# A two-layer graph network on one core: the order of work in layer 0's rounds, in layer 1's node steps, and at the end of both layers

## The chip, the core and the metric

The kernel runs on one core of a Trainium2 chip. The metric is the device time of one execution in microseconds (us); smaller is better. The engines are named as the profile names them: PE (matrix products and transposes), DVE (vector engine), ACT (scalar engine with activation tables), POOL (here it issues the gathers) and SP (it issues nearly all other DMAs). Each engine works through its own instructions strictly in the order in which they were written down, and waits where an operand isn't ready.

## What is computed

6250 nodes with 128 features, 106250 edges sorted by destination. Layer 0 is an attention layer (GATv2), layer 1 a mean of edge messages with a gate. Cut to what matters:

```python
h  = relu(layernorm(x))
xl = h @ Wl + bl ; xr = h @ Wr + br
m  = leaky_relu(xl[src] + xr[dst] + edge_attr @ We, 0.2)
logits = m @ att
ex = exp(logits - segment_max(logits, dst)[dst])
agg = segment_sum(xl[src] * (ex / segment_sum(ex, dst)[dst]), dst)
x  = x + batchnorm(gelu(h + agg + bias_out))          # batch norm: over all nodes

h  = relu(layernorm(x))
em = relu(layernorm(concat(h[src], h[dst]) @ msg_w + msg_b)) * edge_weight
messages = segment_sum(em, dst) / (count + 1e-8)
g  = sigmoid(h @ gate_w + gate_b)
x  = x + g * relu(layernorm(concat(h, messages) @ upd_w + upd_b)) + (1 - g) * h
```

## The kernel before, in words

**Blocks and rounds.** The edges are cut into 104 blocks (`NS`) of 1024 edges, 8 tiles (`ST`) of 128 edges. Both layers run a loop of one round per block `s`. In each round POOL issues eight indirect DMAs (`gather`, L200) that fetch the source rows of 1024 edges from a table in HBM; PE spreads the destination rows to the edges by a product with a one-hot matrix (`expand`, L895; the one-hot comes from `one_hot_t`: a product into `dlp` at L890 and a comparison into `oht` at L891); and a block's sum by destination is again a product with a one-hot matrix (`oh`). That sum is copied out of PSUM and stored to HBM (`flush`, `store` at L898) in one of two tables, by the parity of the block.

**Layer 0's round** (L1056 on). The newest block `s`: DVE adds the gathered rows to the spread rows in PSUM (L1072), ACT takes Relu (L1073), DVE multiplies by the attention vector (L1098), reduces to logits (L1100) and puts them into `lgc` (L1101 to L1104). Behind it, the lagging block `u = s - 7` (`LAG` = 7): its one-hot `oh` (L1079, DVE), the copy of two extra columns (L1082), eight weightings of gathered rows with the softmax numerators (L1094, ACT; after the last gather every second one on DVE, L1092), and the product into `agg_ps` (L1110), which has a single PSUM buffer. `flush(u - 1)` empties that buffer (L1046). Gathered rows have 10 buffers.

**Maxima.** Every fourth round a generator `maxima(b)` (L936) starts. It takes the maximum of the logits over each destination for 4 blocks in eight steps, two per round: a transpose of the logits (L940), scans on DVE (L943 to L948), small transposes (L951, L952), scans of one row, transposes (L966), scans and Exp (L969 to L974), transposes back (L977, L978), and the result `exm` (L982, L984) that the weighting of these 4 blocks reads. Its PSUM tiles share the buffer `mx` with `dlp`.

**Node groups of layer 0** (`nodes`, L989). 13 groups of 4 nodes tiles (the last two have 3 and 2). A group starts when its edges have been stored (`due`), and takes one step per round: load both tables (L904); two empty steps; the maxima and an Exp (L1001 to L1006); the combine and transposes (L1009 to L1022); the bias and Gelu (L1024, L1026); the statistics of the batch norm (L1028). Group 11 starts at round 109; group 12, the last, after the loop. `both(group, nodes(12))` runs the two in turn, one step of each, the last group first. After them come the batch norm's scale (L1150 to L1158, with a Sqrt at L1151), and the stage that makes layer 1's tables.

**Layer 1's round** (L1323 on). DVE adds gathered and spread rows (`y`, L1338); ACT squares the eight tiles with a sum (L1343) and takes Sqrt (L1344); `flush1`; for the block before, `u = s - 1`: one-hot (L1349), scaling (L1354, eight), a bias (L1356) on DVE, Relu (L1357) and weighting (L1360, eight) on ACT; the product into `agg1_ps` (L1370, single buffer). Gathered rows have 6 buffers.

**Node groups of layer 1** (`nodes1`, L1248), again one step per round at the end of the round: load; an empty step; the mean of messages (L1258 to L1266); transposes into `nt` and a copy (L1273, L1274); products into `nz` and, in the same step, their reading into `z` (L1278 to L1281); statistics and Sqrt (L1287 to L1290); scaling (L1292 to L1295); the rest on DVE with transposes of `h` into `nt` and of `x` into `nz` (L1298 to L1311); the output's DMA (L1314). `nt` and `nz` are single buffers of one PSUM bank; `nt` is also the buffer of layer 1's `dlp`. Group 10 starts at round 97, group 11 at round 103, group 12 after the loop; when a group is due, the one before it is finished first, with all the steps that are left.

The order of work is written out by hand (`manual_schedule`): within a layer each engine gets its instructions in the order of the source.

## Time and profile before

| | |
|---|---|
| median of 3 runs | 2320.14 us (2317.82 to 2320.94) |
| time of the profiled execution | 2316.21 us |
| its span, first to last instruction | 2314.1 us |
| granted PE clock, mean | 0.807 |
| busy: POOL, DVE, PE, ACT | 1611.4, 1766.5, 1437.2, 1273.6 us |
| last gather of layer 0 issued at | 1104.39 us |
| first and last gather of layer 1 issued at | 1216.66, 2256.41 us |

How to read the profile. A line of a group reads: line, engine, operation, output<-input, count | busy us, mean ns of one | idle time of the engine just before it, and what ended most of it. A line in order of time reads: start in us, duration in us, engine, line, operation, output<-input, shape, count, and in brackets the idle time before it and its releaser. The busy table by stage has one row per stretch of time: the busy us of PE, PE's weight loads, DVE, ACT and POOL, then the granted PE clock, the share of the DMA engines, and GB/s. Consecutive instructions of one line are merged in the view in order of time.

### The profile page before, as it was taken

The numbers are of one execution on the slowest core, as the hardware profiler recorded it, in microseconds if no ns is written. First come the engines' busy times: TensorE is split into PE (matmuls) and PEld (weight loads), VectorE is DVE, ScalarE is ACT, GpSimd is POOL, SyncE is SP. The second block draws the span as 40 slices with busy tenths as digits, with TensorE's granted clock in tenths as the row PEclk, the third lists the DMA queues.
The fourth block names the chain that finished last, engine by engine and source line by source line (L and its number), as shares of the span: only waits on it lengthen the run. The fifth ranks groups of instructions, "written<-read, shape, count | busy, mean of one in ns | idle before, by whom it ended". The sixth has DMA issues, their size and how long they took to land.

```text
span 2314.1 us, 30585 instructions
## 1 busy us (share of the span) xinstructions
PE 1437.2 (62%) x8206; PEld 1245.6 (54%) x8206; DVE 1766.5 (76%) x3795; ACT 1273.6 (55%) x4208; POOL 1611.4 (70%) x1703
## 2 busy tenths in 40 slices
PE   5656666566656666666585666666665666566663
PEld 4545555455555555556464555555555555555553
DVE  5578788788788788777655777797797887788786
ACT  5224344443344344443465776777777777777674
POOL 1777777777777777777037777777777777777770
PEclk9679878887787878887787777888888788888886
DMA  5742343332332332332132222232233233233231
GB/s 149 179 132 68 87 142 107 76 76 67 76 77 67 76 77 67 77 76 66 40 112 61 67 76 75 70 80 78 68 80 80 64 80 81 66 81 79 67 79 28
DMA packets 187647, 188.13 MB, mean 81 GB/s; under 512 B 38256, under 2 KB 154960, under 8 KB 187464
## 3 DMA queue, kind: packets, MB, share of 16 engines
q0 software_dynamic: 53792, 110.57, 19.8%
q1 hardware_dynamic: 130812, 75.25, 11.3%
q8 instruction: 66, 1.08, 0.2%
q10 hardware_dynamic: 2860, 0.27, 0.1%
q14 instruction: 117, 0.96, 0.1%
HBM read 142.91 MB, written 43.04 MB: 80 GB/s over the span
## 4 chain that ended last, share of the span: by engine, by line
POOL 31%; DVE 25%; issue 14%; DMA 12%; PE 10%; ACT 6%; DVEq 0%; POOLq 0%; ACTq 0%; another core or an unknown queue 0%; SPq 0%
POOL gl L200 31%; DMA gl<-xl_d,src_c 8%; DVE y L1354 4%; DMA gl<-a_d,src_c 3%; PE agg_ps L1370 3%; DVE m_ps L1072 3%; DVE y L1338 2%; DVE oh L1349 2%; DVE y L1356 2%; ACT sq L1343 2%; DVE oht L891 2%; ACT y L1357 1%; ACT glw L1360 1%; PE mm L1203 1%; DVE lr L1100 1%
## 5 line engine op out<-in xcount | busy, mean ns | idle before, releaser
L200 POOL DMA_INDIRECT gl<-xl_d,src_c x832 | 790.6, 950 | 298.8 <-issue 230.4
L200 POOL DMA_INDIRECT gl<-a_d,src_c x832 | 787.4, 946 | 261.0 <-issue 226.2
L1370 PEld LDWEIGHTS agg_ps<-glw,oh 128*128 128x128 f32 x1664 | 314.3, 272 | 481.6 <-ACT glw L1360 481.6
L890 PE MATMUL dlp<-dl_b,ident_b 104*128 104x512 bf16 x416 | 179.3, 431 | 607.4 <-DVE oht L891 500.1
L1110 PEld LDWEIGHTS agg_ps<-glw,oh 128*128 128x128 f32 x1664 | 295.8, 267 | 228.6 <-ACT glw L1094 209.8
L1370 PE MATMUL agg_ps<-glw,oh 128*128 128x129 f32 x1664 | 341.1, 382 | 90.7 <-ACT glw L1360 81.3
L891 DVE TENSOR_SCALAR oht<-dlp,iota_p 126x512 f32<-126x512 f32 x416 | 309.7, 744 | 97.9 <-PE dlp L890 97.9
L1343 ACT ACTIVATE sq<-y 128x128 f32<-128x128 f32 x832 | 256.9, 309 | 225.3 <-DVE y L1338 202.4
L1073 ACT ACTIVATE m_ps<-m_ps 128x1024 f32<-128x1024 f32 x104 | 104.9, 1008 | 501.1 <-DVE m_ps L1072 249.3
L1110 PE MATMUL agg_ps<-glw,oh 128*128 128x130 f32 x1664 | 299.1, 355 | 22.6 <-ACT glw L1094 10.5
L895 PE MATMUL m_ps<-W,oht 128*128 128x128 f32 x1664 | 255.5, 317 | 12.1 <-DMA oht<-in_edge_weight_dram 6.2
L1072 DVE TENSOR_TENSOR m_ps<-m_ps,gl 128x1024 f32<-128x1024 f32 x104 | 128.0, 1231 | 173.6 <-DMA gl<-xl_d,src_c 164.5
L1360 ACT ACTIVATE glw<-y,ew_c 128x128 f32<-128x128 f32 x832 | 254.5, 389 | 3.4
L895 PEld LDWEIGHTS m_ps<-W,oht 128*128 128x128 f32 x1664 | 238.5, 229 | 20.8 <-DVE lr L1100 11.0
L1094 ACT ACTIVATE glw<-gl,exm 128x128 f32<-128x128 f32 x804 | 245.9, 393 | 0.1
L895 PEld LDWEIGHTS y_ps<-W,oht 128*128 128x128 f32 x1664 | 223.4, 216 | 8.9 <-issue 7.2
L895 PE MATMUL y_ps<-W,oht 128*128 128x128 f32 x1664 | 227.0, 295 | 0.0
L1354 DVE SCALAR_TENSOR_TENSOR y<-y,rs,cst 128x128 f32<-128x128 f32 x832 | 223.2, 340 | 0.0
L1338 DVE TENSOR_TENSOR y<-y_ps,gl 128x1024 f32<-128x1024 f32 x104 | 125.3, 1205 | 47.4 <-DMA gl<-a_d,src_c 45.7
L1343 ACT ACTIVATION_READ_ACCUMULATOR sq<-y 128x1 f32 x832 | 155.0, 186 | 0.0
L1357 ACT ACTIVATE y<-y 128x1024 f32<-128x1024 f32 x104 | 109.9, 1056 | 44.2 <-DVE y L1356 44.2
L1100 DVE TENSOR_REDUCE lr<-m_ps 128x8 f32<-128x1024 f32 x104 | 127.3, 1224 | 3.6
(255 smaller groups left out, 1769.2 us busy)
## 6 DMA issues: line engine op xcount, KB each, us to landing
gl<-xl_d,src_c POOLq DMA_INDIRECT x832
gl<-a_d,src_c POOLq DMA_INDIRECT x832
res<-agg SPq DMA_DIRECT2D x104, 64.0 KB
res<-agg SPq DMA_DIRECT2D x104, 63.5 KB
W<-xr_d SPq DMA_DIRECT2D x104, 63.0 KB
W<-b_d SPq DMA_DIRECT2D x104, 63.0 KB
res<-zt SPq DMA_DIRECT2D x20, 325.0 KB
res<-zt SPq DMA_DIRECT2D x20, 322.5 KB
```

What stands on the lines that cost most here:

```text
L200: GP.indirect_dma_start(out=dest, out_offset=None, in_=table, in_offset=bass.IndirectOffsetOnAxis(ap=idx, axis=0))
L890: T.matmul(dlp, ident_b[:NS, s : s + 1].to_broadcast([NS, P]), dl_b[:, es], start=True, stop=True)
L891: V.tensor_scalar(oht[:WIN, es], dlp[:WIN, :], iota_p[:WIN, :], None, op0=ALU.is_equal)
L895: T.matmul(ps[:, j, :], oht[:, j * P : (j + 1) * P], w, start=True, stop=True)
L1072: V.tensor_tensor(ps, ps, gl[:, :, :D], ALU.add)
L1094: S.activation(glw[:, j, :D], glu[:, j, :D], AF.Copy, scale=f)
L1110: T.matmul(aggs[u], oh[:, j, :], glw[:, j, :], start=(j == 0), stop=(j == ST - 1))
L1338: V.tensor_tensor(y, pss.pop(s), gl, ALU.add)
L1343: S.activation(sq, y[:, j, :], AF.Square, accum_out=rs[:, j : j + 1])
L1354: V.scalar_tensor_tensor(yu[:, j, :], yu[:, j, :], ru[:, j : j + 1], mg_ps, op0=ALU.mult, op1=ALU.mult)
L1360: S.activation(glw[:, j, :D], yu[:, j, :], AF.Copy, scale=ew_c[:, u, j : j + 1])
L1370: T.matmul(aggs[u], oh[:, j, :], glw[:, j, :], start=(j == 0), stop=(j == ST - 1))
```

## The change

In layer 0's round the lagging block's one-hot, copied columns, eight weightings and the flush of the block before it now stand ahead of the newest block's add and Relu. The step of `maxima` that stood after the Relu stays there in three rounds of four; in the fourth, the step that makes `exm` follows the lagging block's one-hot. After the Gelu of the last group there is one more ACT instruction: a Sqrt of a constant into a place that is written again later. The two last groups run in an order that is spelled out letter by letter (`in_turn`), where Exp of the last group precedes Gelu of the one before.

In layer 1's node steps the empty step goes; the transposes join the step of the mean; the copy and the products make the next step, and `z` is read from the products one step later, together with the statistics. The transposes of `h` and of `x` are separate steps, each read one step later. All four products now share the buffer `nz`. At the end of layer 1, round 103 only starts the load of group 11; group 10 is finished in round 104, and the last two groups run in a spelled out order.

```diff
-        def both(a, b):
-
-            left = [b, a]
-            while left:
-                for g in list(left):
-                    if next(g, True):
-                        left.remove(g)
+        def in_turn(a, b, order):
+
+            for c in order:
+                next(a if c == "a" else b, None)
+            finish(a)
+            finish(b)
...
                 S.activation(hT_sb[:, ns], hT_sb[:, ns], AF.Gelu)
+                if last:
+                    S.activation(std_c[:, 0:1], eps, AF.Sqrt)
                 yield
...
-            steps, group = None, None
+            steps, group = iter(()), None
...
                 if s + 1 < NS:
                     spread(s + 1)
-                if s < NS:
-                    ps = pss.pop(s)
-                    V.tensor_tensor(ps, ps, gl[:, :, :D], ALU.add)
-                    S.activation(ps, ps, AF.Relu)
-                if steps is not None:
-                    next(steps, None)
                 if 0 <= u < NS:
                     b, q = divmod(u, SB)
                     oh = ep.tile([P, ST, P], F32, name="oh")
                     V.tensor_tensor(oh, over_tiles(iota_ps, ST), over_features(dl_c[:, u, :], ST),
                                     ALU.is_equal)
+                    if q == 0:
+                        next(steps, None)
                     glw = ep.tile([P, ST, W0], F32, name="glw")
                     V.tensor_copy(glw[:, :, D:], exm[b][:, q])
-                if s + 2 < NS:
-                    one_hot_t(ps_1, "mx", s + 2, 0, *wins[s + 2])
-                if u >= 1 and s < NS:
-                    flush(u - 1)
-                if 0 <= u < NS:
                     glu = gls.pop(u)
...
-                if s >= NS:
+                if u >= 1:
                     flush(u - 1)
+                if s < NS:
+                    ps = pss.pop(s)
+                    V.tensor_tensor(ps, ps, gl[:, :, :D], ALU.add)
+                    S.activation(ps, ps, AF.Relu)
+                if u < 0 or u % SB:
+                    next(steps, None)
+                if s + 2 < NS:
+                    one_hot_t(ps_1, "mx", s + 2, 0, *wins[s + 2])
...
                     steps = maxima(s // SB)
-                    next(steps, None)
-                elif steps is not None:
-                    next(steps, None)
+                next(steps, None)
...
-            both(group, nodes(NGR - 1))
+            in_turn(group, nodes(NGR - 1), "baabbbabbab")
...
                 fetch(fin, res1_d, t0, n)
                 yield
-                yield
                 inv = small.tile([P, 2, TN], F32, name="inv")[:, :, :n]
...
-                yield
                 mT = e1.tile([P, m, P], F32, name="mT", tag="mT" + z_)
                 z = e1.tile([P, m, D], F32, name="z", tag="z" + z_)
-                tp = ps_1.tile([P, TN, P], F32, name="nt")
+                tp = ps_1.tile([P, TN, P], F32, name="nt", tag="nz")
                 for j in range(n):
                     T.transpose(tp[:, j, :], fin[:, 0, j, :D], ident)
+                yield
                 S.copy(mT[:, :n, :], tp[:, :n, :])
-                yield
                 zp = ps_1.tile([P, TN, D], F32, name="nz")
...
+                yield
                 for j in range(n):
                     V.scalar_tensor_tensor(z[:, j, :], zp[:, j, :], rstd_c[:, t0 + j : t0 + j + 1],
                                            b1[:, 2 * D : 3 * D], op0=ALU.mult, op1=ALU.add)
-                yield
                 mv = small.tile([P, TN, 2], F32, name="mv1")
...
-                tp = ps_1.tile([P, TN, P], F32, name="nt")
-                xp = ps_1.tile([P, TN, P], F32, name="nz")
-                for j in range(n):
-                    T.transpose(tp[:, j, :], h_sb[:, t0 + j, :], ident)
+                hp = ps_1.tile([P, TN, P], F32, name="nh", tag="nz")
+                for j in range(n):
+                    T.transpose(hp[:, j, :], h_sb[:, t0 + j, :], ident)
+                yield
+                for j in range(n):
+                    V.scalar_tensor_tensor(z[:, j, :], hp[:, j, :], keep[:, t0 + j : t0 + j + 1], z[:, j, :],
+                                           op0=ALU.mult, op1=ALU.add)
+                xp = ps_1.tile([P, TN, P], F32, name="nx", tag="nz")
+                for j in range(n):
                     T.transpose(xp[:, j, :], x_sb[:, t0 + j, :], ident)
-                for j in range(n):
-                    V.scalar_tensor_tensor(z[:, j, :], tp[:, j, :], keep[:, t0 + j : t0 + j + 1], z[:, j, :],
-                                           op0=ALU.mult, op1=ALU.add)
+                yield
                 V.tensor_tensor(z[:, :n, :], z[:, :n, :], xp[:, :n, :], ALU.add)
                 yield
...
-                if s in due:
+                if s in due and s < NS - 1:
                     finish(group)
                     group = nodes1(due[s])
-                if group is not None:
+                if group is not None and s < NS - 1:
                     next(group, None)
-            both(group, nodes1(NGR - 1))
+                if s == NS - 1:
+                    late, last = nodes1(due[s]), nodes1(NGR - 1)
+                    next(late)
+                if s == NS:
+                    finish(group)
+                    next(late)
+            in_turn(late, last, "baaababababa")
```

## The prediction

> **What bounds the kernel now.** I read the page's chain and groups first, then busy time by stage, then the instructions in order of time around the two layer ends.
>
> The page's chain, and its costliest groups (busy us, mean ns | idle before):
>
> ```profile
> POOL 31%; DVE 25%; issue 14%; DMA 12%; PE 10%; ACT 6%; DVEq 0%; POOLq 0%; ACTq 0%; another core or an unknown queue 0%; SPq 0%
> ...
> L200 POOL DMA_INDIRECT gl<-xl_d,src_c x832 | 790.6, 950 | 298.8 <-issue 230.4
> L200 POOL DMA_INDIRECT gl<-a_d,src_c x832 | 787.4, 946 | 261.0 <-issue 226.2
> ```
>
> Busy time by stage (PE, PEld, DVE, ACT, POOL; then granted clock):
>
> ```profile
> 600.00:800.00 200.00, 126.58 (x731) 110.20 (x731) 155.63 (x286) 80.03 (x220) 151.24 (x161) 0.80 0.31 75
> 1700.00:1900.00 200.00, 124.61 (x746) 109.15 (x744) 167.30 (x373) 149.20 (x560) 151.23 (x161) 0.83 0.29 77
> ```
>
> 161 gathers per 200 us in both layers: one starts every 1.25 us (0.95 busy, 0.30 issue) and none waits for another engine. A round is 8 gathers, 9.97 us; DVE is busy 78% and 84% of it. So inside the rounds POOL sets the time and any order that keeps up is free. What can be won lies after each layer's last gather, where POOL is idle. The instructions in order of time, end of layer 0:
>
> ```profile
> 1104.39 0.94 POOL L200 DMA_INDIRECT gl<-xl_d,src_c  x1 [0.30 <-issue]
> 1108.19 1.23 DVE L1072 TENSOR_TENSOR m_ps<-m_ps,gl 128x1024 f32<-128x1024 f32 x1 [4.44 <-DMA gl<-xl_d,src_c]
> 1111.08 3.83 PE L1110 MATMUL agg_ps<-glw,oh 128*128 128x130 f32 x16 [5.73 <-ACT glw L1094]
> 1114.70 0.42 PE L940 MATMUL mx<-ident,lgc 128*32 128x128 f32 x1
> 1115.16 0.28 DVE L943 COPY lt<-mx 32x128 f32<-32x128 f32 x1 [1.59 <-PE mx L940]
> 1132.88 0.24 PE L977 MATMUL tx<-ident,rv 32*128 32x32 f32 x1
> 1147.85 0.27 ACT L1046 COPY agg<-agg_ps 128x130 f32<-128x130 f32 x1 [2.19 <-PE agg_ps L1110]
> 1161.36 0.29 ACT L1151 ACTIVATE bn<-bmv,eps 128x1 f32<-128x1 f32 x1
> ```
>
> The last gather lands at 1108.1, and layer 1's tables can start only at 1161.65: 53.5 us. The same view, end of layer 1:
>
> ```profile
> 2251.34 3.53 PE L1370 MATMUL agg_ps<-glw,oh 128*128 128x129 f32 x16 [2.67 <-ACT glw L1360]
> 2257.00 1.13 DVE L1281 SCALAR_TENSOR_TENSOR z<-nz,rstd_c,b 128x128 f32<-128x128 f32 x4 [7.01 <-PE nz L1279]
> 2258.04 1.21 DVE L1338 TENSOR_TENSOR y<-y_ps,gl 128x1024 f32<-128x1024 f32 x1
> 2265.59 1.23 DVE L1338 TENSOR_TENSOR y<-y_ps,gl 128x1024 f32<-128x1024 f32 x1 [0.22 <-issue]
> 2280.47 1.22 DVE L1349 TENSOR_TENSOR oh<-cst,dl_c 128x1024 f32<-128x1024 f32 x1
> 2290.06 0.27 ACT L1245 COPY agg<-agg_ps 128x129 f32<-128x129 f32 x1 [1.49 <-PE agg_ps L1370]
> 2294.88 0.16 DVE L1258 TENSOR_TENSOR inv<-fin 128x2 f32<-128x2 f32 x1 [1.44 <-DMA fin<-res]
> 2309.42 0.42 DVE L1311 TENSOR_TENSOR z<-z,nz 128x256 f32<-128x256 f32 x1
> ```
>
> DVE stands 7.01 us because group 10's `z` reads products that PE issues behind the round's 16 matmuls; so round 102's `y` (its rows landed near 2249) starts at 2258.04 and round 103's at 2265.59, although its last gather was issued at 2256.41.
>
> **The change part by part**, on the profiled execution's clock (span 2314.1).
>
> *Layer 0's rounds.* Nothing is added: one-hot (1.21), the 16-column copy (0.15), eight weightings (2.44 on ACT) and flush (0.28) go ahead of the add. The store that flush issues on SP comes later by the weighting at most; a group's loads follow rounds later. POOL's queue gets and loses nothing. I cost this at 0, because DVE now does 1.4 us in the wait for the gather (164.5 us over the layer). If that cover failed it would cost about 0.3 us a round, the part of the 1.01 us Relu that the first `oht` (0.74) doesn't hide. DVE per round: 1.21+0.15+1.23+0.74+1.21+1.22+0.4+0.74 = 6.9, plus about 1.0 of maxima steps and 0.6 of node groups, plus that 0.3: 8.8 of 9.97.
>
> *Layer 0's end.* Round 103: one-hot and weighting of block 96 finish at 1106.7, before the gather lands. Its product must now wait for the copy of 95 behind the weighting (1107.0) and ends near 1110.7, not 1114.91. Logits: 1108.19 + 1.23 + 1.01 + 1.21 + 1.22 + 0.35 and small gaps = 1113.4; their transpose runs at 1113.6 instead of 1114.70. But `lt` now stands behind block 97's one-hot, copy and DVE weightings (1.21+0.15+0.87): 1115.65, against 1115.16, a loss of 0.5. Rounds 104 to 106: before, every step, one-hot, weighting and product follow each other, 18.0 us from `lt` to the transposes of L977/L978. After, the 2.2 us of one-hot and weighting lie beside the product of the block before. The path is three products (3.3, 2.4, 2.1), copies of 0.25 and hand-overs: 1115.65 to 1124.35. Round 107's `exm` stands behind a one-hot (+1.1); from there to the last flush it is 14.9 us as before: 1140.5 against 1148.12, **7.6 us**.
>
> Here a rule speaks against the change. Trace: the 16 matmuls of one product took 3.83 at 1111.08 after an idle PE, 2.69 at 1117.55, 2.06 when close together. The Trainium skill, "TensorE: Matmul & The Clock Gate" (section "Why this matters for your kernels"), says that gaps over about 3 us put PE back to half rate. The change makes such a gap (1110.7 to 1114.85). By the row, 2.69 for block 97; by the rule 3.8, so 1.1 us less gain. I take 3.3, and 2.4 and 2.1 for the next two, whose gaps close.
>
> *The node ends of layer 0.* Before, Exp, Gelu, Exp, Gelu, Sqrt each bring a table load: five. After, both Exp go first: three, with Sqrt's behind the last Gelu. Each load is 1.28 in the trace, the next activation starting at once (1148.13 to 1149.43). The Trainium skill, "ScalarE: Activation LUTs" (section "What ACT_TABLE_LOAD costs"), adds a drain of 1.38 to a switch; this trace doesn't show it. Two loads are worth 2.56 by the row, 5.3 by the rule. I follow the row, and not all of it is path, since the second Exp waits for group 12's rows: store and load take 4.8 after the last flush, as before. Then 0.8 (maxima), Gelu's load and two Gelus with group 12's combine between, Sqrt's load, 0.3: 11.85 from flush to Sqrt's end, against 13.5: **1.7 us**.
>
> The stage between the layers is unchanged and moves by 9.3.
>
> *Layer 1's rounds.* Nothing added; `nt` now holds only `dlp`, and four node tiles share the one `nz` bank, each a round apart, so it costs 0 here. The DVE stalls (70.1 us over ten groups) go, but POOL doesn't see them.
>
> *Layer 1's end.* With the stall gone, `y` of 103 waits only for its gather. From issue to landing an ordinary last gather of a round takes 2.5, layer 0's very last 3.72. That one is the nearest row: 2260.1 (or 2258.9), a gain of 5.5 (or 6.7). Block 102's product follows 10.7 later, as before. Group 10's rest (2271.3 to 2280.5 on DVE) no longer stands before block 103's one-hot: that starts at 2266, and the product ends at 2276.2 against 2290.03. What is late next: group 10's `xp` transposes queue behind that product on PE, its output at 2277.5; on SP the store of block 103 waits behind that output's DMA (1.4 us), and behind the store wait the loads of group 12. Their rows arrive at 2282.5, not 2294.88: gain 12.4. On DVE group 11's combine waits for that same `xp`: 2277.5 to 2280.4; before it was done under block 103's product. Then the two groups take turns in one bank: products of 11 until 2283.9 (idle PE), its `z` and statistics until 2286.4, combine of 12 until 2289.1, `hp` of 11 until 2290.6 and read by 2291.75, products of 12 until 2293.95, `xp` of 11, output 11 at 2296; statistics, scaling, `hp`, `xp` of 12 and the last add end at 2300.6. From that add's end to the end of the span was 4.26: 2304.8. From 12's rows to the end is 22.3 against 19.2, so 3.1 is given back: **9.3 us** net. The bank's price I can bound only: if no hand-over delays anything, 1.5 us better; if each of its eight costs 0.4 more, 3 worse. I take the middle, which uses rows already shown.
>
> Sum: 7.6 + 1.7 + 9.3 = 18.6. Span 2314.1 − 18.6 = 2295.5. The profiled execution's time was 2316.21, 2.1 above its span, so 2297.6. The median of the runs is 3.9 above that: 2301.5.
>
> **The rivals.**
>
> *Half the gain (0.17).* One end doesn't shrink: in layer 1 the shared bank and the late combine eat what the earlier `y` brings, or in layer 0 cold products keep the step chain as long as before. For: the trace shows both ends as hand-overs with PE at a low clock; 3.1 us are given back already by my own sum. Against: the 7.01 us stall is a plain wait that goes. 2301.5 + 9.3 = about 2311.
>
> *Slower (0.05).* In layer 0 flush now queues behind eight weightings on ACT, the single `agg_ps` can't be refilled before flush, and the Relu of the new logits stands behind both. Should the loop product → flush → Relu → logits → `oht` → product get longer than POOL's 9.97, each round stretches and after a few rounds the gather buffers run out. Over 104 rounds it decides from 18.6/104 = 0.18 us a round; at 0.35 it gives 2320.1 − 18.6 + 36 = 2338. Against: my count of the loop over two rounds is 17.7 with the longest steps and a slow product, of 19.94.
>
> *No change to be seen (0.05).* The ends are held by loads and stores: each store is followed by a load of its rows, 4.8 us per end whatever the order; if DVE just waits for these earlier, 2317.
>
> **How the numbers follow.** The sum as worked out: 0.73, 2301.5, of itself 2297 to 2306 from the bounds above (landing 1.2, bank −3 to +1.5, product rates ±1.5, and 1.5 of scatter between runs). A measurement of this kernel can tell about 0.2%, 4.6 us, from no change. Half the gain still counts as faster: 0.73 + 0.17 = 0.90. The range reaches to half the gain: 2296 to 2311.
>
> **What the profile would show.** Right: POOL still starts 161 gathers in 200 us; L1281's waits for `nz` nearly gone; about 8.9 us from `lt` to L977 at the end of layer 0; one Sqrt load just behind the last Gelu; last gather of layer 0 to Sqrt's end about 44 us; round 103's `y` within 4 us of its last gather's issue; from that gather's landing to the end about 45. Wrong: POOL waits for ACT or DVE in the rounds; `agg_ps` waits for flush in every round; PE waiting for DVE on the `nz` bank for more than 3 us at the end.

## The result and the profile after

The changed kernel takes 2301.84 us (median of 6 runs, 2294.78 to 2308.34), where the kernel before takes 2321.76 us (median of 6, 2317.82 to 2330.35): ratio 0.9907, 95% interval 0.9881 to 0.9933. The forecast was 2301.5 us. The profiled execution took 2294.78 us with a span of 2293.0 us, 21.1 us less than before's span.

Six of the runs below (e1 to e6) fell on chips where every kernel, the one before too, took about 3200 us: there the gathers waited for VectorE and ScalarE (over 900 us in e1's profile), for a reason that isn't known, so of them only the stretches behind the last block's add are read, and whole times only as ratios.

The page's chain and its costliest groups, after:

```profile
POOL 33%; DVE 25%; issue 16%; DMA 13%; PE 8%; ACT 2%; SPq 0%; DVEq 0%; ACTq 0%; POOLq 0%
...
L200 POOL DMA_INDIRECT gl<-xl_d,src_c x832 | 790.8, 951 | 299.2 <-issue 226.5
L200 POOL DMA_INDIRECT gl<-a_d,src_c x832 | 787.3, 946 | 260.9 <-issue 239.9
```

Busy time by stage, after (PE, PEld, DVE, ACT, POOL; then the granted clock):

```profile
600.00:800.00 200.00, 123.19 (x731) 107.15 (x731) 156.58 (x287) 81.60 (x220) 151.30 (x160) 0.82 0.33 72
1700.00:1900.00 200.00, 127.46 (x739) 113.21 (x738) 164.82 (x371) 148.86 (x556) 151.23 (x161) 0.79 0.31 74
```

The pace of the rounds hasn't changed: 160 and 161 gathers in 200 us, one every 1.25 us. From the first to the last gather layer 0 takes 1043.16 us before and after, layer 1 1039.75 and 1039.14. The gain lies behind the gathers, as it had to. The instructions in order of time at the end of layer 0, after:

```profile
1106.13 0.94 POOL L200 DMA_INDIRECT gl<-xl_d,src_c  x1 [0.30 <-issue]
1109.85 1.23 DVE L1091 TENSOR_TENSOR m_ps<-m_ps,gl 128x1024 f32<-128x1024 f32 x1 [3.85 <-DMA gl<-xl_d,src_c]
1116.42 3.80 PE L1110 MATMUL agg_ps<-glw,oh 128*128 128x130 f32 x16 [0.84 <-DVE glw L1079]
1116.97 0.27 DVE L942 COPY lt<-mx 32x128 f32<-32x128 f32 x1
1125.07 0.24 PE L976 MATMUL tx<-ident,rv 32*128 32x32 f32 x1
1140.36 0.27 ACT L1047 COPY agg<-agg_ps 128x130 f32<-128x130 f32 x1 [2.19 <-PE agg_ps L1110]
1151.24 0.28 ACT L1149 ACTIVATE bn<-bmv,eps 128x1 f32<-128x1 f32 x1
```

The gather lands as late as before (the add starts 3.7 us behind its issue). Then from `lt` to the transposes of L976 it is 8.1 us where it was 17.7: the product at 1116.42 and the two behind it run beside the chain of maxima (`lt` is its first row on VectorE, the transposes of L976 stand near its end). From the add's start to the end of batch norm's square root it is 41.67 us; before it was 53.46.

The end of layer 1, same view:

```profile
2243.13 1.41 POOL L200 DMA_INDIRECT gl<-a_d,src_c  x1 [0.31 <-issue]
2247.80 1.23 DVE L1337 TENSOR_TENSOR y<-y_ps,gl 128x1024 f32<-128x1024 f32 x1 [3.15 <-PE nh L1301]
2264.31 0.27 ACT L1243 COPY agg<-agg_ps 128x129 f32<-128x129 f32 x1 [1.71 <-PE agg_ps L1369]
2264.74 0.69 DVE L1310 TENSOR_TENSOR z<-z,nx 128x512 f32<-128x512 f32 x1 [5.71 <-PE nx L1308]
2272.26 0.87 DVE L1278 SCALAR_TENSOR_TENSOR z<-nz,rstd_c,b 128x128 f32<-128x128 f32 x3 [4.07 <-PE nz L1275]
2288.35 0.42 DVE L1310 TENSOR_TENSOR z<-z,nx 128x256 f32<-128x256 f32 x1 [0.78 <-PE nx L1308]
```

Round 103's `y` starts 4.70 us behind its gather's issue, not 9.19, and from it to the end of the span it is 45.20 us, not 48.51. (The `nh` that the row names has nothing to do with `y`; the trace's landings of the gather end at 2247.72, so the gather was the last.) VectorE's longest waits in layer 1, before and then after (us in total, times, longest):

```profile
DVE z L1281 <- PE nz L1279: 70.1, 10, 7.2
...
DVE y L1338 <- DMA gl<-a_d,src_c: 32.4, 27, 4.1
```

```profile
DVE y L1337 <- DMA gl<-a_d,src_c: 98.6, 60, 4.3
```

The 70.1 us of waits for `nz` are gone, and nearly as much (66.2 us) has come to the waits for the gather: nearly all of the stall was covered by POOL's pace and has only changed its name, except in the last rounds.

Where the 21.1 us came from, stretch by stretch of the two profiled executions ("square root" or "root" is the Sqrt of layer 0's batch norm, the row L1149 above):

| stretch | before | after | difference | forecast |
|---|---|---|---|---|
| start to layer 0's first gather | 61.23 | 62.97 | +1.74 | 0 |
| layer 0, first to last gather | 1043.16 | 1043.16 | 0 | 0 |
| its last gather to the square root's end | 57.26 | 45.39 | −11.87 | −9.3 |
| from there to layer 1's first gather | 55.01 | 52.47 | −2.54 | 0 |
| layer 1, first to last gather | 1039.75 | 1039.14 | −0.61 | 0 |
| its last gather to the end | 57.69 | 49.87 | −7.82 | −9.3 |

The first row is scatter as far as the record shows: the opening is the same code in every kernel, and in the other profiles that took about 2300 us it was 62.2 to 67.0 us.

### The profile page after: what moved, and what is told of

It is laid out like the page before. It is cut to its first block, busy times and chain, and to the rows that moved or that the text cites. A ratio compares the mean times of both kernels' runs of the same rounds, so it can differ in the third digit from the quotient of the medians.

```text
span 2293.0 us, 30473 instructions
## 1 busy us (share of the span) xinstructions
PE 1445.7 (63%) x8206; PEld 1254.5 (55%) x8206; DVE 1769.5 (77%) x3795; ACT 1278.8 (56%) x4207; POOL 1611.8 (70%) x1703
## 4 chain that ended last, share of the span: by engine, by line
POOL 33%; DVE 25%; issue 16%; DMA 13%; PE 8%; ACT 2%; SPq 0%; DVEq 0%; ACTq 0%; POOLq 0%
POOL gl L200 33%; DMA gl<-xl_d,src_c 7%; DMA gl<-a_d,src_c 4%; DVE y L1353 3%; DVE m_ps L1091 3%; DVE oht L891 3%; DVE y L1337 2%; DVE y L1355 2%; DVE oh L1348 2%; DVE lr L1100 2%; DVE m_ps L1098 1%; PE agg_ps L1369 1%; PE m_ps L895 1%; DVE oh L1074 1%; PE mm L1201 1%
## 5 line engine op out<-in xcount | busy, mean ns | idle before, releaser
L1369 PE MATMUL agg_ps<-glw,oh 128*128 128x129 f32 x1664 | 346.5, 389 | 51.6 <-ACT glw L1359 51.6
L1110 PE MATMUL agg_ps<-glw,oh 128*128 128x130 f32 x1664 | 294.3, 350 | 10.5 <-ACT agg L1047 6.8
L895 PEld LDWEIGHTS y_ps<-W,oht 128*128 128x128 f32 x1664 | 230.1, 221 | 8.6 <-issue 6.9
L895 PE MATMUL y_ps<-W,oht 128*128 128x128 f32 x1664 | 233.4, 301 | 0.0
L1098 DVE TENSOR_TENSOR m_ps<-m_ps,att 128x1024 f32<-128x1024 f32 x104 | 127.0, 1221 | 15.3 <-ACT m_ps L1092 15.0
L1356 ACT ACTIVATE y<-y 128x1024 f32<-128x1024 f32 x104 | 109.9, 1056 | 45.3 <-DVE y L1355 45.2
```

What stands on the lines that cost most here:

```text
L895: T.matmul(ps[:, j, :], oht[:, j * P : (j + 1) * P], w, start=True, stop=True)
L1110: T.matmul(aggs[u], oh[:, j, :], glw[:, j, :], start=(j == 0), stop=(j == ST - 1))
L1369: T.matmul(aggs[u], oh[:, j, :], glw[:, j, :], start=(j == 0), stop=(j == ST - 1))
```

## The experiments

All readings in one table, in us of each kernel's profiled execution. "Add to root" is from the start of round 103's add in layer 0 to the end of the square root; "to the copy" is its first part, to the start of the last copy of a product; "between" is from that root to layer 1's first gather; "y" is the start of round 103's `y` after its gather's issue, and "y to end" the rest of the span.

| kernel | layer 0's rounds / end | layer 1's steps / end | add to root | to the copy | between | y | y to end |
|---|---|---|---|---|---|---|---|
| before | old / old | old / old | 53.46 | 39.66 | 55.0 | 9.19 | 48.51 |
| after | new / new | new / new | 41.67 | 30.51 | 52.5 | 4.70 | 45.20 |
| e7 (after again) | new / new | new / new | 41.27 | 30.21 | 52.5 | 4.78 | 44.02 |
| e1 | new / old | old / old | 44.79 | 30.84 | 52.4 | | 48.61 |
| e5 (e1 again) | new / old | old / old | 45.05 | 31.09 | 54.5 | | 48.90 |
| e2 | old / new | old / old | 52.06 | 41.06 | 54.8 | | 48.55 |
| e3 | old / old | new / new | 52.31 | 38.50 | 55.0 | | 44.96 |
| e4 | new / new without one operation | new / new | 43.07 | 30.99 | 51.9 | | 44.11 |
| e6 | new / new | new / old | 41.88 | 30.83 | 54.8 | | 44.70 |
| e8 | one line moved / new | new / new | 43.11 | 31.93 | 52.4 | 4.46 | 44.64 |
| e9 | new / new | better / better | 41.12 | 29.97 | 52.3 | 4.88 | 36.52 |
| e10 | old after the last gather / new | new / new | 50.77 | 39.82 | 54.4 | 4.18 | 44.02 |
| e11 (e6 again) | new / new | new / old | 41.02 | 29.97 | 52.2 | 4.60 | 44.60 |
| e12 | new / new | old / new | 41.53 | 30.45 | 54.5 | 8.78 | 48.12 |

(For e1 to e6 the engines are rounds behind the gathers, so "y" says nothing there. Each row is one profiled execution. "To the copy" is 38.5 to 41.1 in the three kernels with the old rounds, 30.0 to 31.1 in the nine with the new ones; "y to end" is 48.5 to 48.9 in the four with the old node steps and the old end, 44.0 to 45.2 in the eight with the new steps.)

**e1 and e5: layer 0's rounds alone.** The kernel before with the changed kernel's loop over layer 0's rounds; old end of layer 0, old layer 1.

> Only layer 0's rounds are reordered; both layer ends keep the old order of the last two groups, layer 1 is the old one. Theory (one-hot and weighting lie beside the product of the block before, only after the last gather): layer 0's end, from the last gather's issue to the end of the batch norm's Sqrt, falls from 57.3 us by 7.6 to 10, to about 48; rounds stay at 161 gathers per 200 us; layer 1's end stays at 57.7; the time falls by 8 to 10 us, ratio 0.996. Rival (the gain comes from the order of the last groups and the table loads): layer 0's end stays at 55 or more. Rival (flush behind the weighting stretches the rounds): fewer than 161 gathers per 200 us and a longer time.

> The new order of layer 0's rounds alone (old tail of layer 0, old layer 1), a second time, since in the first set every kernel and the kernel before too stood waiting for something outside the core in most rounds. Theory (the gain at layer 0's end comes from the order of the rounds, since the lagging block's weights no longer stand behind the newest block's logits): last gather issue of layer 0 to the end of batch norm's square root falls from 57.3 us to about 48, layer 1's end stays at 57.7, the whole is about 2310 us where the kernel before takes 2320. Rival (the gain is the order of the tail and the square root's table, not the rounds): 57.3 falls by no more than 2, the whole is 2318 to 2320. Beside these: the stretch from that square root to layer 1's first gather took 52.4 us in the two earlier runs with the new rounds and 54.8 to 55.0 in the two with the old ones; if it belongs to the order of the rounds, it is 52.4 again, and the whole nearer 2308; if it is chance it is either.

Measured: add to copy 30.84 and 31.09, as in the changed kernel and 8.6 to 8.8 below before; copy to root 13.95, as before (13.80). So the order of the rounds brings all of the first part and nothing of the second: theory right for the layer's end. The forecast of the whole failed: it was slower there, ratio 1.0118 (1.0049 to 1.0187) and 1.0147 (1.013 to 1.0164), so where the gathers don't cover it, the new order costs. And e1 and e5, the same kernel, took 52.4 and 54.5 from the root to layer 1's first gather: that stretch doesn't belong to the order.

**e2: layer 0's end alone.** The kernel before with

```diff
-            both(group, nodes(NGR - 1))
+            in_turn(group, nodes(NGR - 1), "baabbbabbab")
...
+                if last:
+                    S.activation(std_c[:, 0:1], eps, AF.Sqrt)
```

> Only the end of layer 0 is reordered (the last two node groups with both Exp first, and the Sqrt placed behind the last Gelu); rounds and layer 1 are the old ones. Theory: from the last flush to the end of the batch norm's Sqrt 13.5 us become about 11 (10.9 in the changed kernel), layer 0's end 57.3 becomes about 54.7; the time falls by 2 to 3 us, ratio 0.999. Rival (the table loads and this order carry layer 0's whole gain): layer 0's end falls to 48 or less.

Measured: to the copy 41.06, from the copy to the root 11.00 instead of 13.80, ratio 1.001 (0.9979 to 1.0042). The node ends give 2.8 us by themselves. In e5, with the old end, ScalarE loads a table five times behind that copy (at 1606.01, 1607.53, 1611.96, 1613.47 and 1618.09), the last one behind a wait of 1.05 for batch norm's sums. In e2, in order of time:

```profile
1605.26 1.28 ACT L1013 ACT_TABLE_LOAD   x1
1610.53 1.28 ACT L1033 ACT_TABLE_LOAD   x1
1611.83 0.52 ACT L1033 ACTIVATE h_sb<-h_sb 128x384 f32<-128x384 f32 x1
1614.28 1.28 ACT L1035 ACT_TABLE_LOAD   x1
```

Three loads, each 1.28 as in e5, and the last one stands right behind a Gelu and no longer waits for the sums. The rival (the whole gain of layer 0's end comes from here) is out: the first part stayed at 41.06.

**e4: that early Sqrt taken out.** The changed kernel without the last two lines of the diff above.

> The changed kernel without the Sqrt of a constant behind the last Gelu. Theory: the table load moves behind the statistics as in the kernel before, and the scale's Sqrt ends 0.6 to 0.9 us later: from the last flush to its end about 11.7 instead of 10.9. Rival (the load would start right behind the Gelu in any case, as the other loads do): no change, 10.9.

Measured, in one execution: copy to root 12.08 instead of 11.0 to 11.2, 0.9 to 1.1 us later (0.6 to 0.9 were forecast). So the early Sqrt is worth some 1.0 us of the 2.8; the other 1.8 goes to the new order with its two loads less, and these two weren't run apart.

**e10: in the rounds after the last gather, the old place of the maxima step.**

```diff
+                if s >= NS:
+                    next(steps, None)
                 if 0 <= u < NS:
...
-                    if q == 0:
+                    if q == 0 and s < NS:
                         next(steps, None)
...
-                if u < 0 or u % SB:
+                if s < NS and (u < 0 or u % SB):
                     next(steps, None)
```

> The changed kernel, but in layer 0's rounds after the last gather the step of the group's maxima goes ahead of the lagging block's one-hot and weighting again, as before the change. Theory (the gain at layer 0's end comes from the one-hot and weighting lying beside the maxima chain in these last rounds): from round 103's add to the last copy of a product 38 to 40 us instead of 30.5 to 31, and to the square root's end 49 to 51 instead of 41.7. Rival (it comes from block 97's weights being ready before the last logits, that is from rounds 102 and 103): the first stays under 33, the second under 44.5.

Measured: to the copy 39.82, to the root 50.77; one time, 2309.33 us, where e7's profiled execution took 2293.63. The theory's numbers, though this edit leaves rounds 0 to 103 as they are. The instructions in order of time of e10 (the product is block 97's), then of e7 (the product is block 98's already):

```profile
1116.77 0.28 DVE L950 COPY lt<-mx 32x128 f32<-32x128 f32 x1 [0.45 <-PE mx L947]
1119.15 3.81 PE L1120 MATMUL agg_ps<-glw,oh 128*128 128x130 f32 x16 [2.42 <-DVE glw L1089]
1136.31 0.19 DVE L989 TENSOR_TENSOR exm<-tx,fst_c 128x32 f32<-128x32 f32 x1 [3.31 <-PE tx L985]
```

```profile
1116.07 0.27 DVE L942 COPY lt<-mx 32x128 f32<-32x128 f32 x1
1119.38 2.06 PE L1110 MATMUL agg_ps<-glw,oh 128*128 128x130 f32 x16 [0.21 <-ACT agg L1047]
1125.10 0.18 DVE L981 TENSOR_TENSOR exm<-tx,fst_c 128x32 f32<-128x32 f32 x1
```

In e10 one-hot (at 1117.74 and again at 1123.64), weighting, product and maxima step follow each other, and `exm`, the end of the maxima chain, comes 19.5 us behind `lt`; in e7 9.0. The gain at layer 0's end is made by the few rounds after the last gather, not by the hundred before it.

**e8: the copy of the finished product ahead again.** The changed kernel with `if u >= 1: flush(u - 1)` moved from behind the lagging block's weighting to ahead of its one-hot.

> The changed kernel with one line moved: in layer 0's rounds the copy of the finished product and its store stand ahead of the lagging block's one-hot and weighting again, not behind them. Question: why the new rounds of layer 0 are slower on these chips, where POOL is not the bound. Theory (the loop product, copy, Relu, logits, selection, product has grown because the copy waits behind eight weightings on ScalarE): the stretch from layer 0's first to its last gather falls by 25 to 45 us against the changed kernel of this set, and the whole with it. Rival (the one-hot and the weighting ahead of the newest logits on VectorE and ScalarE do it by themselves): within 10 us of it. At layer 0's end (from the last add to the square root's end) both expect 41.7 within 1.5 us, since there the copy is not late in either order.

This set ran where the kernel before takes 2321.35 us (median of 11), so its question, about rounds in which the gathers don't set the pace, wasn't answered. First to last gather of layer 0: 1044.79 us, against 1043.02 in e7. Add to root 43.11 against 41.27, just inside the forecast of 41.7 within 1.5; the whole 2307.07 (2300.25 to 2311.63), ratio 0.9931 (0.991 to 0.9953), not to be told from e7's.

**e7: the changed kernel again**, in the same set.

> The changed kernel itself on the chips of the experiments, where every kernel, the one before too, takes about 3200 us: in stretches that come only while gathers are being issued, instructions that take 0.03 us on SyncE take 0.7, and the engines fall some rounds behind the gathers. So layer ends are measured from the last block's add, not from its gather. Theory: from round 103's add in layer 0 to the end of batch norm's square root 41.7 to 42 us (before: 52.1 to 53.5), from round 103's y in layer 1 to the end 44.5 to 45.2 (before: 48.5 to 48.9). The whole: layer 0's rounds alone gave ratios of 1.012 and 1.015 here, layer 1 alone 0.984; if the parts add up, the ratio is 0.995 to 1.0. Rival (the parts are not independent: the ends change when both are there): either stretch is off by over 2 us.

2302.39 us (2293.63 to 2307.74), before 2321.35 (2317.31 to 2328.16): ratio 0.9927 (0.9901 to 0.9952). The forecast of the stretches held (41.27 and 44.02); the one of the whole was for other conditions.

**e3: layer 1 alone.** The kernel before with the changed kernel's layer 1.

> Only layer 1 is changed (node steps a round later, the shared bank, the new order of its end); layer 0 is the old one. Theory: layer 1's end, from the last gather's issue to the end of the span, falls from 57.7 us to about 50, layer 0's end stays at 57.3; the time falls by about 8 us, ratio 0.9965. Rival (the two ends depend on each other, or the shared bank eats the gain): layer 1's end at 54 or more. The stretch between the layers can be 52.5 or 55.0 us in any of these runs, by the clock that PE is granted in its first products: if that is right, it takes these two values or ones between without regard to the edit.

Ratio 0.9836 (0.9774 to 0.9898); `y` to end 44.96, as in the changed kernel. Layer 0's stretches are those of the old rounds (52.31 from add to root), so the ends don't depend on each other. The forecast of the whole, 0.9965, was far too small a gain: on these chips the gathers don't set the pace, and what layer 1's new steps save there wasn't taken apart.

**e6 and e11: the new node steps with the old end.**

```diff
-                if s in due and s < NS - 1:
+                if s in due:
...
-                if s == NS - 1:
-                    late, last = nodes1(due[s]), nodes1(NGR - 1)
...
-            in_turn(late, last, "baaababababa")
+            both(group, nodes1(NGR - 1))
```

> The changed kernel with layer 1's old end: its node steps still read TensorE's products a round later, but the last full group is finished in the last round and groups 11 and 12 then run in turn as before, instead of the last full groups a round earlier and a named order for the last two. Theory (layer 1's end gains from the order of the end, not from the later reads): the stretch from layer 1's last gather issue to the end goes back from 49.9 us to between 55 and 58, all else as in the changed kernel, so about 2301 to 2303 where one profiled execution of it gave 2295. Rival (the later reads do it): it stays at 49 to 51. Layer 0's end should be the changed kernel's 45.4 again, within 2 us, and the stretch between the layers 52.4 or 54.5 to 55.0 by the phase of TensorE's clock.

> The changed kernel with layer 1's old end (the last full group finished in the last round, groups 11 and 12 in turn) and the new node steps, a second time; the first time, on a chip where everything took 3200 us, from round 103's y to the end took 44.7 us, as in the changed kernel, and the idea that the order of the end brings the gain had failed. Where the gathers set the pace: theory (the later reads do it all): y of round 103 4.2 to 4.9 us after the last gather's issue, from that y to the end 44 to 45.5, the whole within 3 us of the changed kernel's 2302. Rival (the order of the end counts once the engines wait for gathers, because group 11's rows are then there early): 47 to 49, the whole 2305 to 2306.

My theory of e6 fell at once: `y` to end 44.70, not 52 or more. In e11, where gathers set the pace, `y` starts 4.60 us behind its gather's issue, 44.60 from there to the end, 2300.56 us (2295.58 to 2302.56), ratio 0.9911 (0.9889 to 0.9932). The new order of layer 1's end brings nothing that can be told from the scatter: `y` to end is 44.02 to 45.20 in the six profiles with the new steps and the new order, 44.60 and 44.70 with the old. The rows of e11 show why; group 11's `z` in it and the first instruction on group 12's rows, then the latter in the changed kernel:

```profile
2273.78 0.87 DVE L1286 SCALAR_TENSOR_TENSOR z<-nz,rstd_c,b 128x128 f32<-128x128 f32 x3 [4.91 <-PE nz L1283]
...
2276.21 0.16 DVE L1263 TENSOR_TENSOR inv<-fin 128x2 f32<-128x2 f32 x1 [0.36 <-DMA fin<-res]
```

```profile
2274.98 0.16 DVE L1255 TENSOR_TENSOR inv<-fin 128x2 f32<-128x2 f32 x1
```

In e11 the last product is copied at 2271.28, 22.1 us behind `y` (2249.20) instead of 16.5, and by the trace's landings group 12's rows are there 26.9 us behind `y` instead of 22.7. But VectorE takes group 12 only behind group 11's `z` and statistics, and that `z` stands 24.6 us behind `y` in e11, 24.5 in the changed kernel and 23.3 in e7. So group 12 starts 27.0 us behind `y` in e11, 27.2 in the changed kernel and 26.1 in e7: the rows that come earlier lie waiting.

**e12: the old node steps with the new end.**

> The other half: the changed kernel with layer 1's old node steps (two PSUM banks, products read in the step that issues them) and the new order of the end. Theory (the later reads do it all): VectorE stands for the products of a group again, y of round 103 comes 8 to 9.5 us after the last gather's issue instead of 4.7, and from it to the end 48 to 49, so 2308 to 2310 in all. Rival (the order of the end carries what follows that y): y as late, but 44 to 45.5 from it to the end, 2305 in all. A third case: the new order with two banks is better than both, under 43, since the better version's two banks took 7.5 us off.

`y` 8.78 us behind the issue, 48.12 from there to the end, 2309.72 us (2305.92 to 2311.95), ratio 0.9951 (0.9934 to 0.9967), where nearly all is layer 0's. (The letters of the new order here count the old steps, the empty one among them.) VectorE's longest wait in e12's layer 1, and the first row of group 10's rest behind round 103's `y` (2255.68):

```profile
DVE z L1287 <- PE nz L1285: 75.4, 11, 7.1
```

```profile
2271.70 0.69 DVE L1304 TENSOR_TENSOR z<-z,ug_r 128x512 f32<-128x512 f32 x1 [5.54 <-ACT z L1301]
```

With e11 this settles it between the two halves: the new node steps carry layer 1's gain, and the new order adds at most 0.4 to 0.8 us (48.12 against 48.51 to 48.90 with the old steps and the old order). What in the steps does it is not settled. They read a product one step later, and they also dropped the empty step and joined others, so that a group is further along: in the changed kernel that row of group 10 (L1294) starts 5.4 us ahead of round 103's `y`, in e12 16.0 us behind it, after a wait for ScalarE. No run has the one without the other.

**e9: a version that beats both.** Three moves in the changed kernel:

```diff
-                hp = ps_1.tile([P, TN, P], F32, name="nh", tag="nz")
+                hp = ps_1.tile([P, TN, P], F32, name="nh", tag="nt" if g in (NGR - 3, NGR - 2) else "nz")
...
+                if g == NGR - 3:
+                    xp = ps_1.tile([P, TN, P], F32, name="nx", tag="nt" if g == NGR - 2 else "nz")
+                    for j in range(n):
+                        T.transpose(xp[:, j, :], x_sb[:, t0 + j, :], ident)
                 yield
...
-                if u >= 1:
+                if u >= 1 and s != NS:
                     flush1(u - 1)
...
                     S.activation(yu, yu, AF.Relu)
+                    if s == NS:
+                        flush1(u - 1)
```

(NGR − 3 and NGR − 2 are groups 10 and 11. A step later, where `xp` was made, group 10 now skips it, and group 11's goes to bank "nt".)

> The changed kernel with three moves at layer 1's end: the transposes of h and x of the last two full groups go to two PSUM banks instead of taking turns in one, the last full group but one has its two sets of transposes in one step (so that its sum no longer waits behind block 103's product), and in the last round the copy of block 102's product goes behind the Relu of block 103. Theory (hand-overs in the one bank and the copy ahead of the Relu are on the path): from round 103's y to the end 39.5 to 41.5 us instead of 44.1 to 45.2. Rival (the path is the last block's product, store, loads and the node chain of the last group; the moved steps lie beside it): 43.5 to 45.2. The whole: 4 us of 3200 can hardly be told apart here.

Measured: `y` to end 36.52 us, 7.5 below e7: the theory's direction, but more than its 39.5 to 41.5. 2290.78 us (2286.11 to 2302.21, 4 runs) against e7's 2302.39 on the same chip; ratio to before 0.9885 (0.9846 to 0.9923). The intervals of e7's and e9's ratios overlap (0.9901 to 0.9923), so the whole times alone don't part them; the stretch does, 36.52 against 44.02 to 45.20 in the eight profiles with the new steps. Its end in order of time:

```profile
2259.11 0.69 DVE L1323 TENSOR_TENSOR z<-z,nx 128x512 f32<-128x512 f32 x1
2265.80 0.87 DVE L1286 SCALAR_TENSOR_TENSOR z<-nz,rstd_c,b 128x128 f32<-128x128 f32 x3 [3.23 <-PE nz L1283]
2279.68 0.42 DVE L1323 TENSOR_TENSOR z<-z,nx 128x256 f32<-128x256 f32 x1 [0.78 <-PE nx L1321]
```

Group 10's `xp` is made at 2246.22, before `y` (2247.78), and not behind the product of block 103, so its sum stands 11.3 us behind `y` instead of 16.9 in the changed kernel (2264.74 − 2247.80) and 15.8 in e7; group 11's `z` follows at 18.0 instead of 24.5 and 23.3, and from there to the last add it is 13.9 instead of 16.1. Against e7 that is 5.3 us ahead of this `z` and 2.2 behind it. The three moves weren't run apart, so which of them brings which share isn't shown.

## Why the prediction was right, and where it wasn't

The time was right to 0.3 us, and the bound (POOL's 1.25 us per gather in the rounds, hand-overs behind the last gather) was right. The equality is largely luck, though. The profiled execution gained 21.1 us, not 18.6, and took 2294.78, not 2297.6; the median lies 7.1 above it and not 3.9, and these two misses cancel. Of the 21.1, 20.3 us come from the two ends and the rounds of layer 1, 2.5 from a stretch that I had put at 0, and 1.7 went the other way at the start.

- **The rounds of layer 0 cost nothing**: right where the gathers set the pace (1043.16 us both). My rival "slower" had named the condition, a loop longer than POOL's round of 10 us; where the gathers don't set the pace, e1 and e5 were 1.2 and 1.5% slower than before. The sign I had named for it, `agg_ps` waiting for the flush in every round, came in part: PE waited for that copy at most 32 times in the changed kernel (57.0 us in all) and 7 times before (13.5 us), and POOL's pace covered it. Which part of the loop makes it slower wasn't shown: e8, made for that, ran where the gathers set the pace.
- **Layer 0's end, 7.6 + 1.7**: mechanism right, both terms too small. From the add to the last copy 9.1 was gained (39.66 to 30.51; e5, with the rounds alone, 8.6), where profiles of one order differ by 1.1 us (new) and 2.6 us (old). On the add's clock I had put `lt` at 7.5, measured 7.1; from `lt` to the transposes of L976 8.7, measured 8.1; from there to the end of the last copy 16.1, measured 15.6. So I had each of the three 0.3 to 0.6 us too long. In the first the rows show why: I summed durations, and a VectorE instruction can start up to 0.1 us before the duration of the one ahead has run out (the weightings start at 1116.18 and take 0.87, `lt` starts at 1116.97). In the second the three products took 7.9 us together where I had 7.8, so the hand-overs were shorter; in the third I let the rest after round 107 run "as before", and a wait of 1.30 us ahead of one product fell to 0.40. The node ends gave 2.6 to 2.8 instead of 1.7: e4 and e2 give 1.0 to the early Sqrt and 1.8 to the order with two loads less, of which I had written off most as lying beside the wait for group 12's rows.
- **The rule on TensorE's gaps.** I weighed a product of 2.69 by the row against 3.8 by the Trainium skill, "TensorE: Matmul & The Clock Gate" (section "Why this matters for your kernels"), whose rule is that idle gaps over about 3 us put PE back to half rate, and took 3.3. Block 97's product took 3.80 in the changed kernel's profile, at a granted clock of 0.50, and 3.45 in e7; the next one, at 1.00, 2.06. So the size of 3.8 was nearer. The gap was another than the one I had worked out (1110.7 to 1114.85), since block 96's product took 3.83 too: it was 2.89 us, and the clock had been at 0.50 since 1103.45, ahead of both. In e7, behind a gap of 2.45, shorter than the rule's, the clock fell from 1.00 to 0.50 at 1115.90, while block 97's product ran. That this product is path fits: the 0.35 us between these two profiles come back as 0.30 at the last copy (30.51 and 30.21).
- **The rule on table loads.** For the drain of 1.38 us that the Trainium skill, "ScalarE: Activation LUTs" (section "What ACT_TABLE_LOAD costs"), adds to each switch there is no sign: in e2 the Exp ahead ends at 1610.52, the load starts at 1610.53, takes 1.28, and Gelu follows at 1611.83. The row was right.
- **The stage between the layers, 0**: the edits don't set it, but it moved by −2.5. Its instructions are the same; what differs is when TensorE's granted clock comes up from 0.50 to 1.00. Busy time from 8.4 us behind the root's end on, before and then after:

```profile
1170.00:1180.00 10.00, 10.00 (x43) 7.86 (x43) 4.63 (x15) 6.15 (x17) 3.73 (x2) 0.83 0.33 98
```

```profile
1160.00:1170.00 10.00, 10.00 (x54) 7.98 (x53) 6.19 (x21) 7.52 (x20) 5.50 (x3) 1.00 0.42 129
```

  By the trace's clock record (the two rows have means of 0.83 and 1.00) it rises 11.7 us behind the root before and 6.5 after, with TensorE's first long product at 2.4 in both. The fourteen profiles show that this is all: where the clock rises 5.4 to 6.6 us behind the root (seven of them) the stretch is 51.9 to 52.5 us, where it rises 10.5 to 11.8 us behind it (the other seven) 54.4 to 55.0, and in each of the fourteen the stretch is, within 0.1 us, 49.2 plus half the time to the rise. The same kernel shows either (e1 and e5; e6 and e11), so no edit sets it. Whether the new order makes the shorter one more frequent (seven of ten profiles with the new rounds, none of the three with the old, and not e10's) stays open.
- **Layer 1's end, 9.3**: size nearly right (7.8, and 8.9 in e7), cause half wrong. "`y` waits only for its gather": right, but it came 4.7 us behind the issue instead of 3.72, 1.0 of the 1.5 missing. (By the landings layer 1's own last gather took 3.92 in before's profile, a nearer row than layer 0's, and 4.59 in the changed kernel's.) The step that failed is to take the arrival of group 12's rows for the path, from "Group 10's rest ... no longer stands before block 103's one-hot" to "gain 12.4". The rows did come earlier, 27.4 us behind the last gather's issue instead of 38.4, a gain of 11.0; but nothing waits for them. With the old order (e11) they come 4.2 us later behind `y`, and the end is where it was; with the new order and the old steps (e12) at most 0.8 us is gained. What I took for the order's net 3.8 (9.3 less 5.5) comes with the node steps: 3.5 to 3.9 us from `y` to the end in e3, e6 and e11, as 3.3 and 4.5 in the changed kernel's two profiles. The part of my chain that did hold is what ate the 12.4: group 11's combine behind `xp` of group 10, and two groups in one bank. e9 moved these, with one move on ScalarE, and won 7.5.
- **The rivals.** "Half the gain" and "no change" didn't come: neither end kept its length.

What stays open: what makes the new rounds of layer 0 dearer where the gathers don't set the pace; which part of layer 1's new steps, the later read or the saved steps, brings the gain; why the last gather of layer 1 lands later in some profiles; and why TensorE's clock comes up some 6 us behind the root in one execution and 11 in another.

## What to carry to other kernels

Where one queue sets the pace, read the stretch behind its last item: order there was worth 12 us in layer 0, and the same moves in the rounds only renamed a wait. New node steps took a stall of 7 us off ten rounds, and only the last of these stalls counted, since the queue covered the others. Rows that arrive earlier are worth nothing if the engine reaches them only behind another group's work, as in layer 1. Test an order and the steps that it orders apart, since each can look like the other's gain.

## What the runs showed of the hardware that was not expected

- The granted clock of TensorE came up from 0.50 to 1.00 at 5.4 to 11.8 us behind the same root, and moved a stage of identical instructions by up to 3.1 us, half a microsecond per microsecond. TensorE had then been busy without a gap for 4.2 us in the changed kernel's profile and for 9.3 us in before's. In the clock record of each of the fourteen profiles, every stretch at one clock but the last is a multiple of 3.41 us long (at this place 20.48 at half speed before, 13.65 after).
- The last gather of a layer lands later than most, and not equally. Where VectorE waited for the last gather of a round in layer 0, its add started 2.5 us behind the issue in the median (before; 2.7 in the changed kernel); behind the layer's last gather it is 3.7 to 4.2. In layer 1, in the eight profiles in which gathers set the pace, it lands 3.9 to 4.1 us behind the issue where the issue itself took 0.94 or 0.95 us (before, e10, e12), and 4.4 to 4.8 where it took 1.02 to 1.41. What makes such an issue long wasn't tried.
- The same sixteen matmuls of block 100 took 3.83 and 3.84 us in the changed kernel's two profiles and 2.06 in e9 and e11, behind the same waits; the granted clock was 0.50 in the first two and 1.00 in the others. The last copy came only 0.24 us later for these 1.78 us (e7 against e11, whose products of block 97 took 3.45 and 3.46). A slow product costs only what isn't covered.
